# Four transformer blocks on one core: MLP chunks in fours, and where the odd chunk is computed

## The chip, the core and the metric

The kernel runs on one core of a Trainium2 chip, in FP32. The metric is the device time of one execution in microseconds. Engines are named as the profile names them: PE is TensorE (PEld its weight loads, which overlap its products), DVE is VectorE, ACT is ScalarE, POOL is GpSimd, SP is SyncE, which issues the DMAs. Each engine works through its own list of instructions in order and waits at an instruction until what it needs is there.

## What is computed

The input `x` is 32 sequences of 128 tokens with 144 channels; `cond` has 144 numbers a sequence. Four blocks follow one another:

```python
x = block0(x, cond)    # adaLN transformer block: 16 heads of 9, MLP of 576
x = rotate(x, cond)    # x + (z @ expm(A(cond)) - z) @ U.T, z = x @ U
x = block2(x, cond)    # adaLN transformer block, as below
x = block3(x, cond)    # attention as below, then 4 experts of which each token takes 2

def block2(x, c):
    sh_a, sc_a, g_a, sh_m, sc_m, g_m = split(silu(c) @ W_ada + b_ada, 6)
    h = layernorm(x) * (1 + sc_a) + sh_a
    x = x + g_a * attention(h)            # softmax(q k^T / 3) v, then W_proj
    h = layernorm(x) * (1 + sc_m) + sh_m
    return x + g_m * (gelu(h @ W_fc1 + b_fc1) @ W_fc2 + b_fc2)
```

In `block3` the last line is `x + g_m * sum_e cw[t, e] * (gelu(h @ w1[e] + b1[e]) @ w2[e] + b2[e])`, where `cw` is the softmax over the two largest of four gate logits and 0 for the other experts.

## The kernel before

**Tiles.** A hidden layer is computed transposed: 128 hidden units on the partitions by 512 tokens (the four sequences of a *group*; there are NG = 8 groups). Such a 128 x 512 piece is a *chunk* and fills one bank of PSUM. 144 channels and a bias are 145 rows of contraction, so each chunk is two products into one bank: the *main* one over 128 rows and the *remainder* over 16 rows and the bias. FP32 products take two passes of PE each. The remainder needs only 32 of the array's 128 rows, so remainders of different chunks can stand in different row tiles of the array (`rows4(k)` names rows 32k to 32k+31) and run beside each other. `hR_m` holds the 17 rows four times, once in each row tile; the weights' remainder rows are laid on the host into the row tile that their chunk uses, `m % 3` before the change.

The MLP of the second transformer block (called the second block here, `layer == 1` in the code) has 576 hidden units: chunks 0 to 3, and a half chunk of 64 units that also carries the bias of the second product, at index SHARED of `hid`. The third block (`layer == 2`) handles its four experts in two *pairs*; a pair has nine chunks, of which one holds the last 64 units of both experts and is the shared one. `both` issues mains and remainders of a step: all of one kind, a `yield`, all of the other kind. `fc1` calls it, then loads the gelu table by a small activation (L1035) and applies gelu to each chunk (L1038). `mlp2` makes the second product (`fc2`, L1044) of one sequence and its residual sum. In the third block `moe2_parts` does so for an expert and a sequence (L1204); the shared chunk's hidden units are first multiplied by gate weights on DVE (`shared_by_gate`, L1176), which come by DMA (`gate_rows`, `gate_rows_of`, the buffer `cwb`), and one further product for each pair and sequence (L1210) takes them.

**The order of the work.** It is written out by hand. Work advances in *ticks*, one for each sequence; in a tick three sequences are in different stages of attention. For the sequence `s0`, `scores` makes the plain scores in two halves, whose row maxima DVE takes (`nm`, L931); `largest_T` (L871) transposes `nm` on PE, and `largest` (L876) adds it to q, so that it is subtracted inside the next product. For `s1`, a tick later, `scores` makes the shifted scores, of which ACT takes the exponentials (L935). For `s2`, another tick later, `weigh` (L950) multiplies by the values, ACT copies the result (`on`, L956), and DVE divides it by the sums (`sums_by_blocks`, L975 to L981). Between these stand named gaps, into which `put` places other work; `put2` places the first half of a step (up to its `yield`) in one gap and the second half in another. In the order of a tick:

```python
fill(tick, "a"); fill(tick, "e"); fill(tick, "t")
scores(s0, s1, 0); fill(tick, "stats"); weigh(s2)
fill(tick, "o"); fill(tick, "b0"); fill(tick, "b"); fill(tick, "den"); fill(tick, "pre1")
sums_by_blocks(s2); scores(s0, s1, 1)
fill(tick, "c"); fill(tick, "y1"); fill(tick, "y2"); fill(tick, "y3")
largest_T(s0); largest(s0); fill(tick, "z"); fill(tick, "d"); project_out(s2)
```

The order of issue is the order on each engine. In the second block what a group `n` with first tick `t0` puts into gap "c" thus stands on PE between the last scores and L871: chunks 0 to 2 at `t0 + 8`, chunks 3 and SHARED at `t0 + 9`, and `qk_chunks` (the projections to q and k, three chunks) of the group three later, at `t0 + 10`. Score products use PE in 32-row tiles, four beside each other; mains use the full array.

**Buffers.** Seven PSUM banks go round in order of use (`bank`); the outputs of `weigh` and of L871 have banks of their own. `hid` holds one group's hidden units.

The lines that matter below: L722 (all products of `both`), L871, L876, L919 (scores), L931, L935, L950, L956, L975 to L981, L1035 and L1038 (gelu), L1044, L1176, L1204, L1210.

## Time and profile before

| | us |
|---|---|
| three runs | 1276.01, 1266.53, 1273.7 |
| their median | 1273.7 |
| the profiled execution | 1277.48 |
| its span | 1275.8 |
| PE busy | 1224.7 (96%) |
| DVE busy | 811.5 (64%) |
| ACT busy | 781.1 (61%) |
| POOL busy | 667.4 (52%) |
| mean granted clock of PE | 0.991 |
| table loads of ACT | 117, 1.28 each |

The span is what the profiler records from the first to the last instruction of one execution; the device time holds a little more. A row of the timeline gives start, duration, engine, line, operation, output<-inputs, shape, and the number of instructions drawn together; in square brackets stands how long the engine was idle before it and what it waited for. The timings of matmuls are modelled from records of their start, and a granted clock of 0.50 (PEclk) means that PE ran at half speed in that stretch. The second block runs from some 470 to 790 us, the third from there to the end, with the first block and the preparation of the rotation before.

### The profile page before, as it was taken

Reading aid. Unit: us, or ns where it says so; the run is one execution under the profiler, and the core shown is the slowest. Engines: PE = TensorE matmul, PEld = TensorE weight load, DVE = VectorE, ACT = ScalarE, POOL = GpSimd, SP = SyncE. Lnnn points to the kernel's source line nnn. Section 1 sums busy time; section 2 is a strip of 40 time slices with the busy share of each in tenths; the row PEclk is TensorE's granted clock in tenths of the full one; section 3 lists DMA queues with packets and bytes.
Section 4 is the critical chain, followed back from the end, with each engine's and each line's share of the span. In section 5 each row is a group of like instructions: output and inputs, shape, how many; then the busy total and the mean of one; then the engine's idle time right before and its main releaser. Section 6 shows DMA issues by size and latency. Waiting matters only on the chain.

```text
span 1275.8 us, 35335 instructions
## 1 busy us (share of the span) xinstructions
PE 1224.7 (96%) x13924; PEld 895.4 (70%) x13924; DVE 811.5 (64%) x2540; ACT 781.1 (61%) x1732; POOL 667.4 (52%) x1627
## 2 busy tenths in 40 slices
PE   6889898999989999999999999999999999999998
PEld 5668676778767677777777767767676767677666
DVE  4698888876775466676667666646464646455342
ACT  2567767678786665767666667555656565555441
POOL 5567776756664545454545454736362626261600
PEclk9999998999999999999999999999999999999999
DMA  8301011010013211111121111210101010110110
GB/s 220 84 3 38 2 37 37 2 38 18 23 36 124 60 42 38 46 55 35 50 86 55 56 38 47 103 55 27 55 27 55 27 55 30 53 37 17 37 36 17
DMA packets 53144, 60.74 MB, mean 48 GB/s; under 512 B 5200, under 2 KB 36560, under 8 KB 52720
## 3 DMA queue, kind: packets, MB, share of 16 engines
q1 hardware_dynamic: 52320, 58.01, 15.1%
q8 instruction: 112, 1.84, 0.6%
q10 hardware_dynamic: 656, 0.44, 0.2%
q14 instruction: 56, 0.46, 0.1%
HBM read 44.18 MB, written 13.07 MB: 45 GB/s over the span
## 4 chain that ended last, share of the span: by engine, by line
PE 67%; DVE 5%; ACT 1%; DMA 1%; issue 1%; POOL 0%; SPq 0%; DVEq 0%
PE ps_h L722 19%; PE ps_f L1204 9%; PE ps_s L919 6%; PE ps_w L919 6%; PE ps_o L950 6%; PE ps_qk L722 5%; PE ps_f L1044 4%; PE ps_pj L1014 3%; PE ps_v L722 3%; DVE nm L931 2%; PE ps_f L1210 1%; PE ps_o L871 1%; PE ps_hT_m L691 1%; PE ps_hT_a L691 1%; DVE block L979 0%
## 5 line engine op out<-in xcount | busy, mean ns | idle before, releaser
L931 DVE TENSOR_REDUCE nm<-ps_s 128x4 f32<-128x512 f32 x384 | 246.6, 683 | 93.7 <-PE ps_w L919 80.7
L935 ACT ACTIVATE pr<-ps_w 128x512 f32<-128x512 f32 x384 | 208.6, 595 | 145.5 <-PE ps_w L919 136.8
L919 PE MATMUL ps_s<-kT,qT 32*128 32x256 f32 (+2 forms) x1536 | 233.7, 407 | 0.9 <-ACT kT L851 0.9
L919 PE MATMUL ps_w<-q,kT 32*128 32x128 f32 x3072 | 232.5, 285 | 0.0
L919 PEld LDWEIGHTS ps_w<-q,kT 32*128 32x128 f32 x3072 | 196.6, 188 | 10.0 <-issue 6.3
L1038 ACT ACTIVATE hid<-ps_h 128x512 f32<-128x512 f32 (+1 forms) x224 | 120.5, 591 | 91.4 <-PE ps_h L722 91.0
L919 PEld LDWEIGHTS ps_s<-kT,qT 32*128 32x128 f32 x1536 | 137.3, 186 | 29.2 <-issue 9.4
L1214 DVE SCALAR_TENSOR_TENSOR acc<-ps_f,cwz,acc 128x144 f32<-128x144 f32 x128 | 46.7, 365 | 157.4 <-PE ps_f L1204 87.8
L722 PE MATMUL ps_h<-hM_m,mlps 128*128 128x512 f32 x304 | 144.1, 607 | 0.0
L1000 POOL TENSOR_TENSOR x_sb<-x_sb,res_a 128x144 f32<-128x144 f32 x96 | 47.1, 491 | 145.0 <-DVE res_a L1003 144.2
L950 PE MATMUL ps_o<-pr,vaug 128*32 128x128 f32 x3072 | 104.2, 276 | 0.0
L950 PEld LDWEIGHTS ps_o<-pr,vaug 128*32 128x32 f32 x3072 | 78.4, 110 | 32.7 <-PE ps_w L919 14.4
L722 PEld LDWEIGHTS ps_h<-hM_m,mlps 128*128 128x128 f32 x304 | 53.3, 189 | 67.0 <-issue 66.2
L1044 PE MATMUL ps_f<-mlps,hid 128*128 128x144 f32 x640 | 93.7, 294 | 0.0
L1044 PEld LDWEIGHTS ps_f<-mlps,hid 128*128 128x128 f32 x640 | 82.4, 190 | 8.8 <-issue 4.5
L935 ACT ACT_TABLE_LOAD x57 | 73.1, 1283 | 10.0 <-PE ps_w L919 9.1
L794 POOL TENSOR_SCALAR kT<-kT,cst 128x512 f32<-128x512 f32 x30 | 47.0, 1565 | 61.1 <-ACT kT L776 59.7
L662 POOL TENSOR_SCALAR rs_m_a<-mv_m_a 128x2 f32<-128x2 f32 x81 | 17.2, 212 | 114.2 <-DVE mv_m_a L660 86.3
L1204 PEld LDWEIGHTS ps_f<-mlps,hid 128*128 128x128 f32 x512 | 67.3, 190 | 13.5 <-issue 12.2
L1204 PEld LDWEIGHTS ps_f<-pair,hid 128*128 128x128 f32 x512 | 68.7, 193 | 9.7 <-issue 7.9
L1035 ACT ACT_TABLE_LOAD x58 | 74.4, 1283 | 1.0
L1204 PE MATMUL ps_f<-pair,hid 128*128 128x144 f32 x512 | 74.5, 292 | 0.0
(337 smaller groups left out, 2725.8 us busy)
## 6 DMA issues: line engine op xcount, KB each, us to landing
gates<-gates SPq DMA_DIRECT2D x48, 288.0 KB
hD_m<-hG_m SPq DMA_DIRECT2D x24, 256.0 KB
hR_m<-hD_m SPq DMA_DIRECT2D x24, 256.0 KB
hD_a<-hG_a SPq DMA_DIRECT2D x16, 256.0 KB
hR_a<-hD_a SPq DMA_DIRECT2D x16, 256.0 KB
cwb<-cwD SPq DMA_DIRECT2D x32, 128.0 KB
x_sb<-in_x SPq DMA_DIRECT2D x8, 288.0 KB
out_x<-x_sb SPq DMA_DIRECT2D x7, 288.0 KB
```

Source lines behind the costliest of these rows:

```text
L722: nc.tensor.matmul(ps, x, y, start=k == 0, stop=k == 1)
L794: eng.tensor_scalar(o, k, m, None, ALU.mult)
L919: nc.tensor.matmul(o, x, y, start=True, stop=True)
L931: nc.vector.tensor_reduce(to, view, AX.X, ALU.max, negate=True)
L935: nc.scalar.activation(pr[:, 4 * e : 4 * e + 4, :].rearrange("p s q -> p (s q)"), view, AF.Exp, scale=SCALE,)
L950: nc.tensor.matmul(po[rows4(j), t, :], v[:, 4 * j + 2 * t + r, :], prs[j // 2][:, 4 * (j % 2) + 2 * r + t, :], start=r == 0, stop=r == 1,)
L1000: nc.gpsimd.tensor_tensor(x_sb[:, b, :], x_sb[:, b, :], t, ALU.add)
L1035: nc.scalar.activation(t, half, AF.Gelu_apprx_tanh)
L1038: nc.scalar.activation(hid[:n, i], ps[:n], AF.Gelu_apprx_tanh)
L1044: nc.tensor.matmul(ps, hid[:, at0, i, :], w2[:, m, :], start=m == 0, stop=m == NFC - 1)
L1204: nc.tensor.matmul(ps[:, 0, :], hid[:, at0 + m, i, :], w2[:, at0 + m, :], start=m == 0, stop=m == 3)
L1214: nc.vector.scalar_tensor_tensor(acc, ps[:, 0, :], w, acc, ALU.mult, ALU.add)
```

## The change

The change has three parts.

**Second block.** `both` gets a third form (`rest_first` is None): half of the mains, then all remainders (which end the first half's banks and begin the second half's), the `yield`, then the other mains. Chunks 0 to 3 are made in one such step at `t0 + 8`. The shared chunk goes into the step of q and k at `t0 + 10` (`JOIN` tells which group's): its main and q's, four remainders, two mains, its gelu, then the copies of q and k. The step at `t0 + 9` goes. The second products of the four sequences move from ticks 10, 10, 11, 11 (gaps b, d, b, c) to 10, 11, 11, 11 (gaps d, b, c, d). `MLP_TILES` names each chunk's row tile, now with the fourth among them.

**Third block.** For the second pair of groups 0 to 4 the nine chunks are made as two steps of four and, for the shared one, in the step of q and k of the group three later. Groups 5 to 7, which no later q and k follow, and all first pairs stay in threes.

**Last group.** For its first pair all shared products are made with the second expert (before, and still elsewhere, `e % 2 == (i == 0)`: sequence 0's with the second expert, the other three with the first), `shared_by_gate` moves from "stats" to "den", and the request for the second pair's gate rows moves, for every group, from "den" to "pre1" behind it.

In the steps of the new form the gelu table is loaded by an activation issued ahead of the products.

```diff
+MLP_TILES = {
+    "L0": (0, 1, 2, 0, 1), "L2": (0, 1, 2, 3, 3),
+    "L3_0": (0, 1, 2, 0, 1, 2, 0, 1, 2), "L3_1": (1, 2, 3, 3, 0, 1, 0, 2, 3),
+}
...
     def both(main, rest, rest_first):
+        if rest_first is None:
+            n = len(main) // 2
+            for ps, x, y in main[:n]:
+                nc.tensor.matmul(ps, x, y, start=True, stop=False)
+            for k, (ps, x, y) in enumerate(rest):
+                nc.tensor.matmul(ps, x, y, start=k >= n, stop=k < n)
+            yield
+            for ps, x, y in main[n:]:
+                nc.tensor.matmul(ps, x, y, start=False, stop=True)
+            return
...
+    JOIN = {(1, n): (1, n - 3) for n in range(3, NG)}
+    JOIN.update({(2, n): (1, n + NG - 3) for n in range(3)})
+    JOIN.update({(2, n): (2, n - 3) for n in range(3, NG)})
+
     def qk_chunks(g):
...
+        f = JOIN.get(g)
+        if f is not None:
+            l, mlp, m = ("L2", MLPS[1], 4) if f[0] == 1 else ("L3_1", PAIRS[1], 3)
+            name = f"{f[0]}_{f[1]}_s"
+            gelu_table(name, m)
+            psh, main, rest = fc1_products(f, l, mlp, name, (m,))
+        else:
+            main, rest = [], []
...
+        main += [(ps, p.wqk[:, c], hM) for ps, c in zip(pss, cols)]
+        rest += [(ps, p.wqkR[rows4(m), cols[m]], hR[rows4(m)]) for m, ps in enumerate(pss)]
+        yield from both(main, rest, False if f is None else None)
+        if f is not None:
+            gelus(f, psh, (SHARED,))
         nc.scalar.copy(qT[:, 0, :], pss[0])
...
+    def fc1(g, l, p, name, ms, to, rest_first):
+        if rest_first is None:
+            gelu_table(name, ms[0])
+        pss, main, rest = fc1_products(g, l, p, name, ms)
+        yield from both(main, rest, rest_first)
+        if rest_first is not None:
+            gelu_table(name, ms[0])
+        gelus(g, pss, to)
...
-        shared = e % 2 == (i == 0)
+        shared = e % 2 == (i == 0 or (g[1], e // 2) == (NG - 1, 0))
...
             elif layer == 1:
-                put2(t0 + 8, "c", "c", mlp1, g, 0, (0, 1, 2), True)
-                put2(t0 + 9, "c", "c", mlp1, g, 3, (3, SHARED), True)
+                put2(t0 + 8, "c", "c", mlp1, g, 0, (0, 1, 2, 3), None)
                 for i in range(G):
-                    put(t0 + (10, 10, 11, 11)[i], "bdbc"[i], mlp2, g, i)
+                    put(t0 + (10, 11, 11, 11)[i], "dbcd"[i], mlp2, g, i)
...
-                put(t0 + 9, "den", gate_rows_of, g, 1)
+                put(t0 + 9, "pre1", gate_rows_of, g, 1)
...
-                    put2(at_, "stats", "b0", moe1, g, pair, 0, True)
+                    if pair and n < NG - 3:
+                        put2(at_, "stats", "b0", moe1, g, pair, 3, None)
+                        put2(at_ + 1, "stats", "b0", moe1, g, pair, 4, None)
+                    else:
+                        put2(at_, "stats", "b0", moe1, g, pair, 0, True)
                     if n == NG - 1:
                         put2(at_, "stats", "pre1", moe1, g, pair, 1, True)
-                    else:
+                    elif not pair or n >= NG - 3:
                         put2(at_, "den", "pre1", moe1, g, pair, 1, False)
-                    put2(at_ + 1, "stats", "b0", moe1, g, pair, 2, True)
-                    put(at_ + 1, "stats", shared_by_gate, g, pair)
+                    if not pair or n >= NG - 3:
+                        put2(at_ + 1, "stats", "b0", moe1, g, pair, 2, True)
+                    put(at_ + 1, "den" if (n, pair) == (NG - 1, 0) else "stats", shared_by_gate, g, pair)
...
-    def mlp(name, w1, b1, w2):
+    def mlp(name, w1, b1, w2, tiles):
...
-            k, cols = m % 3, slice(128 * m, 128 * m + 128)
+            k, cols = tiles[m], slice(128 * m, 128 * m + 128)
```

`fc1_products` collects the banks, mains and remainders that `fc1` made itself before; `gelu_table` and `gelus` hold its two uses of ACT.

More of the change, by code (lines that the diff above doesn't have):

```diff
@@ L759, in qk_chunks @@
         qT, kT = qk_tiles(g)
+        f = JOIN.get(g)
[6 more added lines that the diff above has]
+            main, rest = [], []
         pss = [bank([128, G * T], f"ps_qk_{g[0]}_{g[1]}_{m}") for m in range(3)]
         cols = [slice(128 * m, 128 * m + 128) for m in range(3)]
-        yield from both(
-            [(ps, p.wqk[:, c], hM) for ps, c in zip(pss, cols)],
-            [(ps, p.wqkR[rows4(m), cols[m]], hR[rows4(m)]) for m, ps in enumerate(pss)],
-            False,
-        )
+        main += [(ps, p.wqk[:, c], hM) for ps, c in zip(pss, cols)]
[3 more added lines that the diff above has]
+            gelus(f, psh, (SHARED,))
         nc.scalar.copy(qT[:, 0, :], pss[0])
@@ L1019, in project_sum, with fc1_products, gelu_table, gelus @@
         residual(b, st[s].pop("pj"), gr[g]["ga"][:, i, :], f"a_{s}", layer == 0)
-    def fc1(g, p, name, m, to, rest_first):
+    def fc1_products(g, l, p, name, ms):
         hM, hR = gr[g]["hM_m"], gr[g]["hR_m"]
-        pss = [bank([128, G, T], f"ps_h_{name}_{m + i}") for i in range(len(to))]
-        cols = [slice(128 * (m + i), 128 * (m + i) + 128) for i in range(len(to))]
-        tiles = [rows4((m + i) % 3) for i in range(len(to))]
-        yield from both(
-            [(ps, p.w1[:, c], hM) for ps, c in zip(pss, cols)],
-            [(ps, p.w1R[r, c], hR[r]) for ps, c, r in zip(pss, cols, tiles)],
-            rest_first,
-        )
+        pss = [bank([128, G, T], f"ps_h_{name}_{m}") for m in ms]
+        cols = [slice(128 * m, 128 * m + 128) for m in ms]
+        tiles = [rows4(MLP_TILES[l][m]) for m in ms]
+        main = [(ps, p.w1[:, c], hM) for ps, c in zip(pss, cols)]
+        rest = [(ps, p.w1R[r, c], hR[r]) for ps, c, r in zip(pss, cols, tiles)]
+        return pss, main, rest
+    def fc1(g, l, p, name, ms, to, rest_first):
[6 more added lines that the diff above has]
+        gelus(g, pss, to)
+    def gelu_table(name, m):
         t = small.tile([128, 1], F32, tag="gelu", name=f"gelu_{name}_{m}", bufs=1)
         nc.scalar.activation(t, half, AF.Gelu_apprx_tanh)
+    def gelus(g, pss, to):
         for ps, i in zip(pss, to):
@@ L1047, in mlp1 @@
     def mlp1(g, m, to, rest_first):
-        return fc1(g, MLPS[g[0]], f"{g[0]}_{g[1]}", m, to, rest_first)
+        ms = range(m, m + len(to))
+        return fc1(g, ("L0", "L2")[g[0]], MLPS[g[0]], f"{g[0]}_{g[1]}", ms, to, rest_first)
     def mlp2(g, i):
@@ L1168, in moe1 @@
     def moe1(g, pair, part, rest_first):
-        to = ((0, 1, 2), (SHARED, 3, 4), (5, 6, 7))[part]
-        return fc1(g, PAIRS[pair], f"3_{g[1]}_{pair}", 3 * part, to, rest_first)
+        ms = range(3 * part, 3 * part + 3)
+        if part > 2:
+            ms = ((0, 1, 2, 4), (5, 6, 7, 8))[part - 3]
+        to = [(0, 1, 2, SHARED, 3, 4, 5, 6, 7)[m] for m in ms]
+        return fc1(g, f"L3_{pair}", PAIRS[pair], f"3_{g[1]}_{pair}", ms, to, rest_first)
     def shared_by_gate(g, pair):
@@ L1625 @@
         w2 = np.vstack([w2, b2, pad[:63, :1].repeat(C, 1)])
-        mlp(l, np.hstack([w1, pad[:C]]), np.hstack([b1, pad[C]]), w2)
+        mlp(l, np.hstack([w1, pad[:C]]), np.hstack([b1, pad[C]]), w2, MLP_TILES[l])
     for n in range(2):
@@ L1635 @@
         w2 = np.vstack([w2[0][:512], w2[1][:512], w2[0][512:], w2[1][512:]])
-        mlp(f"L3_{n}", w1, b1, w2)
+        mlp(f"L3_{n}", w1, b1, w2, MLP_TILES[f"L3_{n}"])
     arrays["L3_b2"] = inputs["L3_cond_b2"].ravel()
```

## The prediction

> **What bounds the kernel now.** I read the page's busy shares first, then the forty slices, then the timeline of one group of the second block, and last the windows of 3.41 us around every half clock.

> ```profile
> PE 1224.7 (96%) x13924; PEld 895.4 (70%) x13924; DVE 811.5 (64%) x2540; ACT 781.1 (61%) x1732; POOL 667.4 (52%) x1627
> ...
> PE   6889898999989999999999999999999999999998
> ...
> PEclk9999998999999999999999999999999999999999
> ```

> TensorE sets the time: 96% over all, and in the windows view 263.4 us of the 265 from 470 to 735 and 349.2 of the 350 from 820 to 1170. So every microsecond that PE gains or waits there is one of the span. The second block's ticks repeat to hundredths of a microsecond, so one group prices eight. Group 0 (start us, duration, engine, line, output<-inputs, count):

> ```profile
> 514.38 1.07 PE L722 MATMUL ps_h<-hR_m,mlps 32*128 32x512 f32 x6
> 515.38 2.84 PE L722 MATMUL ps_h<-hM_m,mlps 128*128 128x512 f32 x6
> ...
> 518.06 0.27 PE L871 MATMUL ps_o<-cst,nm 128*128 128x128 f32 x1
> ...
> 524.48 0.28 PE L919 MATMUL ps_w<-q,kT 32*128 32x128 f32 x2
> ...
> 524.59 1.02 PE L722 MATMUL ps_h<-hR_m,mlps 32*128 32x512 f32 x4
> ...
> 524.97 1.28 DVE L931 TENSOR_REDUCE nm<-ps_s 128x4 f32<-128x512 f32 x2
> ...
> 525.55 1.98 PE L722 MATMUL ps_h<-hM_m,mlps 128*128 128x512 f32 x4
> ...
> 527.37 0.27 PE L871 MATMUL ps_o<-cst,nm 128*128 128x128 f32 x1
> ...
> 534.17 2.84 PE L722 MATMUL ps_qk<-hM_a,L_wqk 128*128 128x512 f32 x6
> ...
> 536.94 1.14 PE L722 MATMUL ps_qk<-hR_a,L_wqkR 32*128 32x512 f32 x6
> ...
> 538.01 0.33 PE L871 MATMUL ps_o<-cst,nm 128*128 128x128 f32 x1
> ```

> See three steps, each between the last score and L871, which stands behind it on PE: chunks 0 to 2 (remainders, mains), chunks 3 and 4 the same way a tick later, q and k (mains, remainders) in the third tick. See also DVE's nm, which L871 transposes: it ends at 526.25, and the second step hides it until 527.37. In group 6 nothing is hidden any more; L871 starts 0.15 after nm:

> ```profile
> 745.26 1.28 DVE L931 TENSOR_REDUCE nm<-ps_s 128x4 f32<-128x512 f32 x2
> ...
> 746.69 0.30 PE L871 MATMUL ps_o<-cst,nm 128*128 128x128 f32 x1
> ```

> **PE's work in the second block.** 2.84 against 1.98 us for six and four passes makes 0.43 a pass, two passes a chunk. The last scores of the three ticks start at 514.31, 524.49 and 533.97, so the steps take 3.75, 2.88 and 4.04. A step of two mains, four remainders, two mains: 0.20 into the full array (533.97 to 534.17), 2.77 - 0.86 = 1.91 for four passes to the remainders, a round of remainders 1.07 (536.94 to 538.01), 1.82 for four passes behind remainders (525.55 to 527.37): 5.00. The fourth remainder in the round is unseen: two chunks' round takes 0.96 and three chunks' 1.00, so a fourth in its own rows costs 0.04 or so, and 0.96 at most, if it runs alone; I take it in the 1.07, as scores run in four row tiles already. So the first step costs +1.25 and q and k +0.96. One of the four second products (L1044) moves from between weigh and the scores to a tick's end (1.43 there, 1.24 among full-array matmuls): -0.19; bound 0. Two short waits of before (0.15 for a bank in tick 11, 0.2 for q in tick 12) stand where PE's work moves later, or earlier; they may go (-0.35) or stay (0); I take the gain. Per group 1.25 + 0.96 - 0.19 - 0.35 = +1.67, times 8: **+13.4** (bounds +12 with a free fourth remainder, +18 with no gain, +32 with the fourth alone in both steps too).

> Against this the step of chunks 3 and 4 goes: 2.88 less the 0.20 of the next change of form is 2.68, times 8 is 21.5. But its place stays empty, and **what is late next is nm**. The last score ends at 524.76, and the reduction of its banks alone takes 1.28. In the trace DVE reaches it at 524.97, after the chain exp, `on`, oT of the sequence ahead, none of which the change touches in this tick. L871 can go at 526.25 + 0.15 = 526.40, only 0.97 before now. The same sum for the other groups (L871 now less nm's end less 0.15): 0.97 for groups 0 to 3, 0.42 for 4, 0.01 for 5, none for 6 and 7, where `on` comes later still. Gain 4.3 in place of 21.5. PE then stands for 1.64 us in groups 0 to 3, 2.2 in 4, 2.6 in 5 to 7. Second block: 13.4 - 4.3 = **+9.1**; bounds +8, +13 and +28 by the ends above; the far one only if a fourth row tile did not run beside three.

> **The clock.** These stalls are more than their length. The clock record changes on a fixed grid of 3.413 us (columns: window, PE busy, weight loads, DVE, ACT, POOL, PEclk, DMA, GB/s):

> ```profile
> 69.48:72.89 3.41, 2.19 (x15) 1.44 (x15) 3.27 (x13) 2.05 (x6) 1.12 (x5) 1.00 0.02 5
> 72.89:76.31 3.42, 2.64 (x60) 2.03 (x59) 3.04 (x12) 2.67 (x8) 2.03 (x5) 1.00 0.00 0
> ...
> 380.10:383.51 3.41, 2.13 (x22) 1.51 (x20) 3.17 (x16) 0.33 (x2) 1.57 (x5) 1.00 0.00 0
> 383.51:386.92 3.41, 3.41 (x48) 3.07 (x52) 3.09 (x12) 1.54 (x3) 2.15 (x7) 0.50 0.02 5
> ...
> 1240.25:1243.66 3.41, 1.25 (x10) 1.16 (x10) 1.80 (x5) 0.00 (x0) 0.00 (x0) 1.00 0.12 39
> 1243.66:1247.07 3.41, 3.41 (x16) 3.41 (x15) 1.45 (x5) 0.00 (x0) 0.00 (x0) 0.50 0.23 82
> ```

> All five windows with 1.28 us or more of idle PE (1.28 at 380, 1.53 at 322, 1.68 at 209, 1.93 at 162, 2.16 at 1240) are followed by one at 0.50; none with 1.22 or less is. A stall of 1.64 leaves 1.28 in one window unless the grid cuts it near the middle: its first part between 0.36 and 1.28, 0.92 of 3.41, so 0.73 of the cases; 0.9 for 2.2, all for 2.6. That is 4 x 0.73 + 0.9 + 3 = 6.8 windows. A half-clock window full of PE work loses 1.7; as some of what follows L871 is short and waits anyway, I take 1.45 (bounds 0 and 1.7): **+10** (0 to 14).
> [...]

> **Third block.** Groups 0 to 4, pair 1: the steps of three chunks (3.73) in two ticks become steps of four (+1.27 each), the step of the other three goes (-3.42), q and k gets its chunk (+0.96): +0.1 a group, bounds -0.4 and +1; L871 has 3.5 us of cover where a step goes, so no stall. ACT gets two more table loads a group, 10 x 1.283 = 12.8 us; its 61% leaves room, the loads stand where ACT waits for PE (bounds 0, +12.8). I take 0 for these: **+0.4**. In the second block the count of loads is the same; one now stands behind q and k's gelu, in front of tick 11's exps: `on` 1.1 later, but DVE there waits for PE's second product until 544.1, just when `on` comes (0 to 0.1). SP's queue keeps its order; the second expert pair's gate rows are asked for one gap later and are wanted a tick after; the residual sums that DVE and POOL do for the moved product are wanted by the next block many ticks on: 0.

> **The tail.**

> ```profile
> 1241.75 0.69 DVE L1176 TENSOR_TENSOR hid<-hid,cwb 128x512 f32<-128x512 f32 x1 [2.64 <-DMA cwb<-cwD]
> 1242.50 0.51 PE L1210 MATMUL ps_f<-pair,hid 128*128 128x144 f32 x2 [2.16 <-DVE hid L1176]
> ```

> The first shared product of the last group waits 2.16 us for a gate row, and the window after runs at 0.50. With the shared products an expert later they are first wanted near 1243.1, and hid is there at 1242.44: -2.16, and -1.7 of the clock: **-3.9** (bounds 0, if the wait only moves, and -4).

> **Sum.** 9.1 + 10 + 0.4 - 3.9 = +15.6. The profiled execution took 1277.5 (span 1275.8 and 1.7 around it), so 1293; it lies 3.8 above the median of the runs, and on that the forecast is **1289**.

> **Rivals.** (1) The stalls come, the clock doesn't fall: +5.6, 1279. For it: the stalls are short and in two windows each. Against: five of five. (2) Other side: L871 finds nm done, because DVE reaches the reduction in time in tick t0+9 of every group; the place is DVE's queue between oT and nm. Then 17.2 more is gained, no window halves, 13.4 - 21.5 + 0.4 - 3.9 = -11.6: 1262. It decides from nm ending at 524.5, 1.7 sooner, and the last scores end only at 524.76; for it speaks that the ends of matmuls are modelled, and the slack of over 1 us at the other ticks. (3) The third block's table loads hold its exps and through them weigh: all of 12.8 on top, +28, 1302. Against: ACT has 39% idle; for: exps release weigh, which PE reaches in order.

> **How the numbers follow.** Forecast 0.55 (+9 to +22, three quarters of it over 1%, which is 12.7 us and about what a measurement here can tell), rival 1 0.25 (+2 to +9, within 1%), rival 2 0.12 (half of it over 1%, as its sum ends 1.1 short), rival 3 0.08 (slower). Slower 0.41 + 0.08 = 0.49; within 1% 0.14 + 0.25 + 0.06 = 0.45; faster 0.06. The range leaves out rival 2 and the far part of rival 3: 1270 to 1298, its low end for the wait at the tail gone and no fall of the clock with cheaper steps.

> **What would show it.** After: L871 in ticks t0+9 of the second block with an idle of 1.6 to 2.6 us put down to DVE's nm, eight times; seven or so windows at 0.50 behind them; steps of 5.0 between last score and L871; no wait at L1210 near 1242. No such wait at L871 makes rival 2 right, waits without half clocks rival 1, waits of L950 for exps in the third block rival 3. The forecast is wrong if four remainders together take far more than 1.07, or if the wait at L871 lets a later wait of PE vanish that I left in place.

## The result and the profile after

| | before | after |
|---|---|---|
| median, us (6 runs each) | 1274.7 (1266.5 to 1276.3) | 1290.7 (1285.5 to 1296.2) |
| profiled execution, its span | 1277.5, 1275.8 | 1295.8, 1294.0 |
| mean granted clock of PE | 0.991 | 0.977 |

The changed kernel takes 1.0139 times as long (95% interval 1.0099 to 1.0178). The forecast was 1289, 1.2% slower. The busy shares and slices of the page after:

```profile
PE 1228.9 (95%) x13924; PEld 898.0 (69%) x13924; DVE 810.0 (63%) x2540; ACT 799.4 (62%) x1742; POOL 664.8 (51%) x1627
...
PE   6889888999989999999999998999999999999998
...
PEclk9689999999999999999999899999999999999999
```

PE's work is the same number of instructions and 4 us more; the span has grown by 18. So the loss is waiting and clock, and neither is large enough in any one slice to catch the eye. The timeline of the second block's tick t0+9 in group 0 shows it (start, duration, engine, line; in brackets the idle time before and what ended it):

```profile
526.76 0.28 PE L944 MATMUL ps_w<-q,kT 32*128 32x128 f32 x2
...
527.32 1.27 DVE L956 TENSOR_REDUCE nm<-ps_s 128x4 f32<-128x512 f32 x2
...
528.74 0.30 PE L896 MATMUL ps_o<-cst,nm 128*128 128x128 f32 x1 [1.71 <-DVE nm L956]
```

L896 is the transposition that was L871 before (the new lines shift all below). Behind the last scores PE has nothing but it, and it stands for nm. The view of PE's waits, 465 to 840 us (us in total, times, longest):

```profile
PE ps_o L896 <- DVE nm L956: 20.6, 17, 2.7
```

In the kernel before the same view from 400 to 735 us has:

```profile
PE ps_o L871 <- DVE nm L931: 1.0, 3, 0.5
```

The eight long waits of the changed kernel are 1.71 four times, 2.18, 2.67, 2.65 and 2.66. The windows of the clock around three of them (window, PE busy, weight loads, DVE, ACT, POOL, PEclk, DMA, GB/s):

```profile
565.81:569.22 3.41, 1.70 (x30) 1.37 (x25) 2.56 (x5) 1.68 (x4) 1.68 (x4) 1.00 0.00 0
569.22:572.63 3.41, 3.41 (x34) 2.86 (x30) 1.25 (x5) 0.56 (x2) 0.48 (x1) 0.50 0.27 77
606.77:610.18 3.41, 1.94 (x16) 1.54 (x16) 2.55 (x8) 2.14 (x5) 0.79 (x2) 1.00 0.00 0
610.18:613.59 3.41, 3.41 (x82) 2.94 (x82) 2.59 (x9) 1.37 (x3) 0.49 (x1) 1.00 0.36 103
760.36:763.77 3.41, 1.00 (x22) 0.81 (x18) 3.31 (x10) 1.63 (x4) 2.78 (x7) 1.00 0.01 2
763.77:767.18 3.41, 3.17 (x22) 2.89 (x26) 0.82 (x3) 1.23 (x3) 0.49 (x1) 0.50 0.08 24
```

The wait of group 1 falls whole into a window and the next one runs at half speed; that of group 2, just as long, is cut by a border (1.47 idle) and costs no clock. Five of the eight waits are followed by half clock, one of them for two windows: six windows.

To see where time goes I take the start of L871 (L896) in each of the 96 ticks from both traces and follow the difference. It is +1.1 us at 418 us, ahead of everything that was changed; then:

| stretch of the program | forecast | measured between the traces |
|---|---|---|
| second block (to the last moved product) | +19.1 | +22.9 |
| third block | +0.4 | -1.6 |
| tail | -3.9 | -4.2 |
| sum | +15.6 | +17.1 |

The same differences serve for the experiments below. They tell what a step costs to some hundredths of a microsecond where neither the clock's windows nor the landing of a DMA falls otherwise; where they do, the sums move: over the second block two executions of one and the same program (the changed kernel and the last run below) differ by 1.0 us. Whole times tell less, since what lies ahead of 418 us differs by -7.3 to +3.2 us between the profiles of this study.

### The profile page after: what moved, and what is told of

It reads as the page before. It is cut to its first block, busy times and chain, and to the rows that moved or that the text cites. A ratio compares the mean times of both kernels' runs of the same rounds, so it can differ in the third digit from the quotient of the medians.

```text
span 1294.0 us, 35350 instructions
## 1 busy us (share of the span) xinstructions
PE 1228.9 (95%) x13924; PEld 898.0 (69%) x13924; DVE 810.0 (63%) x2540; ACT 799.4 (62%) x1742; POOL 664.8 (51%) x1627
## 4 chain that ended last, share of the span: by engine, by line
PE 66%; DVE 5%; ACT 2%; issue 1%; DMA 1%; POOL 0%; DVEq 0%; SPq 0%
PE ps_h L735 11%; PE ps_f L1242 10%; PE ps_s L944 6%; PE ps_w L944 6%; PE ps_o L975 5%; PE ps_f L1078 4%; PE ps_pj L1039 3%; PE ps_h L731 3%; PE ps_h L726 3%; PE ps_v L735 2%; DVE nm L956 2%; PE ps_qk L731 2%; PE ps_h L728 2%; PE ps_f L1248 1%; PE ps_h_s L726 1%
## 5 line engine op out<-in xcount | busy, mean ns | idle before, releaser
L1072 ACT ACTIVATE hid<-ps_h 128x512 f32<-128x512 f32 (+1 forms) x211 | 114.8, 595 | 67.6 <-PE ps_h L735 61.2
L975 PE MATMUL ps_o<-pr,vaug 128*32 128x128 f32 x3072 | 107.1, 281 | 0.0
L1078 PE MATMUL ps_f<-mlps,hid 128*128 128x144 f32 x640 | 92.9, 292 | 0.0
L706 ACT ACTIVATE hM_m<-ps_hT_m,modM 128x128 f32<-128x128 f32 x96 | 44.5, 463 | 75.8 <-PE ps_hT_m L695 66.7
L1242 PE MATMUL ps_f<-mlps,hid 128*128 128x144 f32 x512 | 72.8, 288 | 0.2 <-ACT hid L1072 0.2
```

The costliest lines, as they stand in the source:

```text
L975: nc.tensor.matmul(po[rows4(j), t, :], v[:, 4 * j + 2 * t + r, :], prs[j // 2][:, 4 * (j % 2) + 2 * r + t, :], start=r == 0, stop=r == 1,)
L1072: nc.scalar.activation(hid[:n, i], ps[:n], AF.Gelu_apprx_tanh)
L1078: nc.tensor.matmul(ps, hid[:, at0, i, :], w2[:, m, :], start=m == 0, stop=m == NFC - 1)
L1242: nc.tensor.matmul(ps[:, 0, :], hid[:, at0 + m, i, :], w2[:, at0 + m, :], start=m == 0, stop=m == 3)
```

## Experiments

### Work in the wait

```diff
+    def fill_pe(tick, count):
+        ot = st[at_tick[tick - 2]]["ot"][:, 3 * T : 4 * T]
+        for _ in range(count):
+            nc.tensor.transpose(ot, ident, ident)
...
                 put2(t0 + 8, "c", "c", mlp1, g, 0, (0, 1, 2, 3), None)
+                put(t0 + 9, "y3", fill_pe, t0 + 9, (12, 12, 12, 12, 16, 20, 20, 20)[n])
```

> The changed kernel with 12 to 20 needless transpositions of a constant on PE (0.11 us each) put ahead of L871 in the ticks t0+9 of the second block; they write where L871 then writes, nothing is left out. Theory (nm is what L871 waits for, and the idle stretch behind which the clock halves is that wait): the extra 1.3 to 2.2 us of work a group lie inside the waits, L871 starts when it did, waits of 0.4 to 0.5 us remain, no window at 0.50 follows them, and the kernel is some 9 us FASTER than the changed one (about 1282, +7 to +8 against the kernel before). Rival (the half clocks have another cause, or the work delays L871): same as the changed one to +13 us slower (1291 to 1304), with half windows as before.

Measured: 1283.6 us median, 1.0082 (1.0050 to 1.0113) of the kernel before: 7 us faster than the changed kernel, by work that nobody needs (the two intervals just overlap; the traces agree with 7.2 us in the second block). The timeline of group 0's tick t0+9:

```profile
521.66 1.53 PE L1093 MATMUL ps_o<-cst 128*128 128x128 f32 x12
...
522.02 1.27 DVE L956 TENSOR_REDUCE nm<-ps_s 128x4 f32<-128x512 f32 x2
...
523.35 0.33 PE L896 MATMUL ps_o<-cst,nm 128*128 128x128 f32 x1 [0.16 <-DVE nm L956]
```

L896 follows the end of the reduction (523.30) as before; the tick is no longer for it (0.08 shorter). No window between 400 and 1280 us runs at 0.50. Against the changed kernel the second block is 7.2 us shorter. That is not yet the price of the clock, for in the ticks behind the waits, those of q and k, another thing differs too: how late `hR_a`, which three of the four remainders there read, comes by DMA. With the filler in group 7:

```profile
797.49 1.12 PE L728 MATMUL ps_h_s<-hR_m,mlps 32*128 32x512 f32 x2
799.39 1.13 PE L728 MATMUL ps_qk<-hR_a,rotU 32*128 32x512 f32 x6 [0.78 <-DMA hR_a<-hD_a]
```

From the first remainder to the next main this round takes 2.96 us, in the changed kernel 1.32. Taken out tick by tick (us, filler less changed kernel):

| group | its q and k tick | of that the round of remainders | what is left | half-clock windows that are gone |
|---|---|---|---|---|
| 0 | -0.94 | -0.94 | 0.00 | 0 |
| 1 | -1.59 | -0.04 | -1.55 | 1 |
| 2 | 0.00 | 0.00 | 0.00 | 0 |
| 3 | -1.60 | -0.03 | -1.57 | 1 |
| 4 | +0.68 | +0.76 | -0.08 | 0 |
| 5 | -2.14 | +0.53 | -2.67 | 2 |
| 6 | -1.04 | +0.41 | -1.45 | 1 |
| 7 | +0.09 | +1.64 | -1.55 | 1 |

So the clock cost some 8.8 of the 22.9 us, 1.5 a window, and it was the waits that set it off. The other 14 are there without it.

### The parts alone

The second block alone has `JOIN` without its third line (the third block's own entries), the third block's pairs and the tail as before; the other two likewise keep one part of the change and undo the rest.

> The kernel before with the change of the second block alone. Theory: all of the loss is here, waits of L871 of 1.7 to 2.7 us in eight ticks and five or six windows at 0.50: +22 us against the kernel before (+18 to +26, by how the grid of windows falls). Rival (part of the loss is ACT's ten added table loads in the third block, or the joint step there): +10 to +16.

> The kernel before with the change of the third block alone (second pair of groups 0 to 4 in fours, the shared chunk with q and k). Theory from the trace after: PE work falls by 0.4 us a group, so -2 us (-4 to 0). By the prediction's sum +0.4. Rival, that the ten added table loads delay exponentials: up to +13.

> The kernel before with the last group's later shared products alone (and its multiplication by the gate rows and the later request for them). Theory: the wait of 2.16 us at the first shared product goes and the window at 0.50 behind it: -3.9 us (-3 to -4.5). Rival, that only the wait goes and the clock still halves, or the wait moves to a later product: -2.2 or 0.

| kernel | median, us | ratio to before | from the traces, us |
|---|---|---|---|
| second block alone | 1300.4 | 1.0194 (1.0151 to 1.0237) | +25.4 |
| third block alone | 1271.7 | 0.9995 (0.9965 to 1.0025) | -1.6 |
| tail alone | 1271.8 | 0.9977 (0.9949 to 1.0005) | -4.1 |

The second block carries the whole loss. Its waits are the same to the tenth as in the changed kernel; seven windows at 0.50 and not six came of them, as the grid fell otherwise. PE's waits there, 400 to 840 us (L895 is L871 of the kernel before):

```profile
PE ps_o L895 <- DVE nm L955: 20.6, 17, 2.7
```

The third block gains 0.4 us in each of groups 0 to 3: the tick in which one step of three goes, one becomes a step of four and the shared chunk joins q and k is 1.28 shorter, the next, with another step of four for one of three, 0.95 longer, and the rest of the group is level (-0.07). In group 4 nothing is gained (-1.28 and +1.29). The ten added table loads of ACT (1.28 each) cost nothing that a tick shows. At the tail neither a wait at the shared product nor a window at 0.50 behind it is left. In the third block's own run, where the tail is as before, the wait is there too (PE's waits, 1200 to 1265 us; L1247 is L1210 of the kernel before), yet a border cuts it (1.64 idle in the window) and no half clock follows:

```profile
PE ps_f L1247 <- DVE hid L1213: 2.0, 1, 2.0
```

So of the tail's gain of 4.1 about half is the wait and half hung on how the grid fell in the profiled execution of before. Neither of these two kernels alone is clear of noise in whole times.

### The table load ahead of the scores

```diff
         gelus(g, pss, to)
+        if l == "L2":
+            t = small.tile([128, 1], F32, tag="gelu", name=f"exp_{name}", bufs=1)
+            nc.scalar.activation(t, half, AF.Exp)
```

> The changed kernel with one small exponential behind the gelus of the step of four in the second block, so that ACT loads the exp table in tick t0+8 and not in t0+9 behind the first scores. Theory (in t0+9 the chain to nm is scores, exp table load, exps, on, oT, reduction, and in groups 0 to 3 the end of the last scores stands right behind it): on comes 1.28 us sooner; L871's wait goes from 1.71 to 1.5 in groups 0 to 3 only, as the reduction cannot begin before the last scores, and from 2.2 to 2.7 down to 1.4 to 1.5 in groups 4 to 7: 5 us faster than the changed kernel, and a few windows at 0.50 less (-5 to -10; 1281 to 1286). Rival (the load is not in the chain, ACT was free for it): waits as before, 0.

Measured: 1292.7 us, 1.0146 (1.0112 to 1.0179) of before, nothing won. Group 0's ticks t0+8 and t0+9 in its timeline:

```profile
512.27 0.27 PE L896 MATMUL ps_o<-cst,nm 128*128 128x128 f32 x1
...
513.09 1.28 ACT L1066 ACT_TABLE_LOAD   x1
...
514.84 0.57 ACT L1100 COPY xM<-ps_xT 128x512 f32<-128x512 f32 x1
514.99 0.98 PE L735 MATMUL ps_v<-L_wvR,hR_a 32*128 32x144 f32 x4
...
519.89 1.29 DVE L956 TENSOR_REDUCE nm<-ps_s 128x4 f32<-128x512 f32 x2 [0.21 <-PE ps_w L944]
521.33 0.30 PE L896 MATMUL ps_o<-cst,nm 128*128 128x128 f32 x1 [1.43 <-DVE nm L956]
```

The first half of the expectation holds: DVE now waits for the last scores (0.21), and L896's wait is 1.43, which is the reduction (1.29) and the 0.15 from its end to L896 alone. No order of ACT makes it less. But the load moved in front of ACT's copies of the tick before, for one of which the weight loads of the values' products wait (0.18): of the four in the row above the last two start at 515.46, 0.05 after the copy of `xM` ends. PE stands there, and the tick t0+9 is 0.65 us longer than in the changed kernel. In groups 4 to 7 the waits stayed at 2.4 to 2.8: there it isn't the load that makes nm late. What does, I have not followed up.

### A tick later, with cover in every tick

```diff
-                put2(t0 + 8, "c", "c", mlp1, g, 0, (0, 1, 2, 3), None)
-                for i in range(G):
-                    put(t0 + (10, 11, 11, 11)[i], "dbcd"[i], mlp2, g, i)
+                if n == 0:
+                    put2(t0 + 8, "c", "c", mlp1, g, 0, (0, 1), True)
+                    put2(t0 + 9, "c", "c", mlp1, g, 2, (2, 3), True)
+                else:
+                    put2(t0 + 9, "c", "c", mlp1, g, 0, (0, 1, 2, 3), None)
+                for i in range(G):
+                    if n < NG - 1:
+                        put(t0 + (11, 11, 12, 12)[i], "bccc"[i], mlp2, g, i)
+                    else:
+                        put(t0 + (10, 11, 11, 11)[i], "dbcd"[i], mlp2, g, i)
```

> The changed kernel with the second block's step of four a tick later (t0+9 in place of t0+8), and the second products of each group in t0+11 (b, c) and, two of them, in gap c of t0+12, which is the next group's t0+8: so every tick has work of PE between the last scores and L871. Group 0 makes chunks 0 to 3 in two steps of two (t0+8, t0+9), the last group keeps its second products. Third block and tail as in the changed kernel. Theory: no wait of L871 over 0.5 us and no window at 0.50 in the second block; PE's sum a group is 0.3 to 0.7 below the kernel before, so -2 to -5 there, with -1.6 in the third block and -4.1 at the tail: 8 to 11 us faster than the kernel before, 1263 to 1267. Rival (the fours lose by themselves, by their round of remainders and its bank): second block +3 to +6, so 1271 to 1275.

Measured: 1277.2 us, 1.0022 (0.9997 to 1.0047) of before, so 13 us better than the changed kernel and not better than before. The long waits and the half clocks are gone as expected. The gain of PE's work is not there: in the traces the second block is 7.0 us longer than before. PE's waits, 400 to 840 us:

```profile
PE ps_qk L728 <- DMA hR_a<-hD_a: 2.5, 4, 1.0
PE ps_o L896 <- DVE nm L956: 2.3, 5, 0.7
PE ps_xR L1103 <- POOL xt L1100: 1.6, 3, 0.5
```

In groups 1 and 2 the four ticks change by -0.99, +2.91, -0.35 and -1.35, together +0.22. PE now comes to the rotation's transpositions some 0.7 us before POOL has what they read, and in the joint step one remainder is late by 0.36 (next section). Without these two the group would gain 0.8. In the other groups the joint step itself is what loses: `hR_a` lands late there, and the round of remainders takes 2.3 to 3.2 us. Over the eight groups these rounds are 10.1 us longer in sum than with 1.07 each, more than the whole 7.0. So the rival was right in its sign and in naming the round of remainders; but what makes it long is mostly an input that comes too late for a step that now comes sooner. By this sum the block would else be 3 us shorter, as the theory had it, though no run shows that.

Third block and tail without the second block's change:

> The changed kernel without the second block's change (third block and tail alone). Theory: the two add up, -1.6 and -4.1: 5.7 us faster than the kernel before, about 1268.5. Rival (the tail's window at 0.50 comes back by another wait, or one part was the noise of the clock): 0 to -2.

Measured: 1271.8 us, 0.9981 (0.9960 to 1.0002) of before; from the traces -1.5 and -4.2, together -5.7. By the traces it is the best of the versions run. Its median lies 19 us under the changed kernel's, but whole times do not tell it from either of its parts alone, and against the kernel before its interval still touches 1.

### The late remainder of the joint step

In the changed kernel the round of remainders at t0+8 takes 1.07 us as forecast (517.44 to 518.51 in group 0), but with q and k 1.30 longer in group 0, 0.40, 0.36 and 0.39 in groups 1 to 3, 0.56 in group 4. Group 1 in the timeline:

```profile
576.49 1.28 DVE L956 TENSOR_REDUCE nm<-ps_s 128x4 f32<-128x512 f32 x2
...
576.81 0.69 PE L728 MATMUL ps_h_s<-hR_m,mlps 32*128 32x512 f32 x1
...
576.82 1.10 PE L728 MATMUL ps_qk<-hR_a,L_wqkR 32*128 32x512 f32 x3
...
578.28 1.98 PE L731 MATMUL ps_qk<-hM_a,L_wqk 128*128 128x512 f32 x4
```

Of the second line's three, two start with the shared chunk's at 576.82 and the third at 577.23, 0.05 after the first of the two reductions ends (577.17). Group 0 and group 4 wait for `hR_a` instead, which lands late there, since the step now comes sooner (`[0.18 <-DMA hR_a<-hD_a]` behind 1.3 us in which only the shared chunk's remainder runs). I took the link to the reduction for the bank: seven go round, and a step of four takes the one that the first scores had.

```diff
+        swap = n == 1 and None not in (s, w) and s // B == 1 and s % G == 2
...
+            if swap:
+                pw = [bank([128, 4 * T], f"ps_w_{w}_{n}_{e}") for e in range(2)]
             ps = [bank([128, 4 * T], f"ps_s_{s}_{n}_{e}") for e in range(2)]
```

> The changed kernel, with one thing other: in the second block's ticks of q and k the second half of the scores takes its four PSUM banks in the order shifted scores, plain scores (before: plain, shifted). The joint step's fourth bank is then one that ACT's exponentials read, which are done 1.5 us sooner than DVE's reductions. Theory (the round of remainders there takes 1.42 and not 1.07 in groups 1 to 3 because the third of q and k, whose bank is the first of the scores, waits for the first reduction): the round falls to 1.07 in groups 1 to 3, so -0.3 to -0.4 in each of these ticks of the trace; groups 0 and 4, where hR_a lands late, keep what that costs. Rival (a fourth remainder from another tile takes that long by itself): rounds of 1.42 as before.

One execution: 1295.1 us. The rounds stay at 1.43 in groups 1 and 2, and the third remainder of q and k again starts 0.05 after the reduction (614.10 after 614.05). But this run is no test of the bank. Its built program is that of the changed kernel, instruction for instruction and bank for bank: the order in which the source asks for these tiles does not decide which bank each gets. So it is a second execution of the changed kernel.

The built program does say which bank it is: in all eight joint steps of the second block the third product of q and k writes the bank that the first plain scores of the tick's second half had, as supposed, and it waits there for a semaphore of DVE's. The traces agree. In the six runs with this step in the second block the third remainder starts with the others where the first reduction is done by then, and 0.05 to 0.06 after its end where it is not (20 times, four each in the changed kernel and with the filler). A run that gives this product another bank would settle it; there is none.

## Why the prediction was right

- **What is late next.** The forecast's main step, that with chunks 3 and SHARED gone L871 would stand for nm, came to within 0.1 us: waits of 1.64, 2.2 and 2.6 forecast from PE's last score, 1.71, 2.18 and 2.66 measured. In groups 0 to 3 the tick of the step that went is 0.91 shorter, where 0.97 was forecast and 2.68 would have been PE's work. The filler run shows it by the other side: work put there costs nothing.
- **The clock.** Right in kind, nearly right in the price of a window (1.45 forecast, some 1.5 measured), and by luck in their number. The forecast had 6.8 windows, from a threshold of 1.28 us of idle PE in a window; six came, and cost some 8.8 us. The threshold was wrong. Over ten traces, past 100 us and ahead of PE's last product, all 25 windows at full clock with 1.65 us of idle or more were followed by half clock, and of 38 with 1.25 to 1.64 fourteen were, ten of which are one place (near 380 us) in every run. With 1.65 and the waits as they came out the same sum gives some five windows. Rival 1, that such short stalls leave the clock alone, has fallen: in groups 1 and 3, where no border cuts the 1.71 us, half clock followed. The reading that no window with 1.22 us of idle or less is followed by half clock overlooks one, at 212.84 us, with 0.76; it is itself at half clock (see the last section).
- **The sum of PE's work** in the second block was too low: +9.1 forecast, some +14 measured without the clock. Mis-sized was the round of four remainders. "I take it in the 1.07" held at t0+8 in groups 0 to 5, and in the joint step in group 5 alone; the trace of before could not show it, as the row I priced it by had three chunks of one kind with their input long there. These rounds are 4.4 us longer over the eight groups (3.7 in the joint step, 0.7 at t0+8 in groups 6 and 7), which is all but some 0.6 us of the error. In groups 1 to 3 the sum is off by as much as the round is (0.70 forecast without the clock, 1.06 measured, the round 0.36 to 0.40 longer), but not because every other term was right. The short wait in tick 11 that was to go (0.14 at L871, and the profile puts it down to nm, not to a bank) is now 0.26, and the second product that moved was worth 1.6 at its old place and not 1.43; such errors cancel.
- **Third block.** +0.4 forecast, -1.6 measured: the lower of the bounds given, -0.4 a group, in four groups, and 0 in the fifth. No sign of the table loads (rival 3) in any tick.
- **Tail.** -3.9 forecast, -4.2 measured, for both reasons given.
- **Rival 2**, that L871 finds nm done, is out: with DVE waiting for nothing but the scores the wait is still 1.43.

Three errors, -1.2 on the clock, +5.0 on PE, -2.3 on third block and tail, took one another back to within 1.5 us. The total was better than its terms, and that is luck.

## What to carry to other kernels

Before a step is taken off an engine that is busy all the time, look at what stands behind it in that engine's queue and when its inputs are there: the step is worth only the slack of that, here 0.97 of 2.68 us and nothing at all in three groups. Fewer, larger steps can have the same fault: here they left a gap empty where small ones had covered a chain through two other engines. And a row that prices a step holds only as long as its inputs come as early: here the joint step, moved ahead in time, met a DMA and a reduction that were not yet done, and its remainders took 0.36 to 1.30 us more than the 1.07 they were priced at, in groups 0 to 4.

## What was not expected of the hardware

In windows at half clock less idle was followed by another. Over the ten traces the six windows at 0.50 with 0.54 us of idle or more were followed by another at 0.50, and the 39 with 0.30 or less by full clock; that is how one wait cost two windows.

Needless matmuls were worth having here: 12 to 20 transpositions of a constant in each of eight waits made the kernel 7 us faster.
